# Four fused convolution layers on one Trainium2 core: other products placed elsewhere between an automaton's steps, and the parts of three pipelined layers in another order

## The chip, the cores and the metric

The kernel runs on one core of one Trainium2 chip. The metric is device time in microseconds (us) of one launch. TensorE is written PE, VectorE DVE, ScalarE ACT, GpSimd POOL and SyncE SP, as in the profile. SP and POOL issue the DMAs here. All matrix products are float32 with 512 columns unless said otherwise; the hardware runs such a product as two passes, and the profile counts passes.

## The reference

The input is 32 images of 8 channels and 256 by 256 pixels. Four layers follow one another, each as `x = x + layer(_gn(x))`, where `_gn` normalises over 4 groups of 2 channels.

```python
# layer 0: an automaton (a coupled map lattice), a small network, and a gate between them
grid = drive = x[:, :8]
for _ in range(15):
    mapped = 3.9 * grid * (1.0 - grid)
    local = conv3x3(mapped, K_local, groups=8)
    grid = 0.85 * (0.7 * mapped + 0.3 * local) + 0.15 * drive
cml = clip(grid, 0.0001, 0.9999)
nca = sigmoid(conv1x1(relu(conv3x3(x, Wp)), Wu))          # 8 -> 128 -> 8 channels
g = sigmoid(conv1x1(relu(conv3x3([x, cml, nca], Wg1)), Wg2))
out0 = g * cml + (1 - g) * nca
# layer 1: 3x3 convolution of values rounded to 127 steps; the scale needs the maximum over all images
# layer 2: 3x3 convolution with bias;  layer 3: 5x5 box filter per channel
```

Layer 1's scale is a maximum over the whole batch, so layer 0 has to be done for all images before layer 1 starts.

## The kernel before

**First part, layer 0.** One image after another goes through `lattice(b, ahead)`, which runs the automaton, and beside it a generator `gated()` makes everything else of layer 0 (the network and the gate) in small batches. The order of all instructions is written out by hand: inside `tc.manual_schedule()` every engine executes in the order in which the Python code emits.

The automaton keeps six of the eight channels on PE. A step handles them as three pairs (j = 0, 1, 2). For each pair PE multiplies the patch of each channel (`patch_sb` with `state`, L408, two products) and then the rim of each patch (`rings`, L410, two products that run side by side); DVE adds the drive in PSUM (L418); ACT squares the sum into the next `state` (L435). `spread(i)` then copies the rims of the patches into `rings` by twelve small DMAs on SP (L272): `spread(0)` after pair 1 for pairs 0 and 1, `spread(1)` after pair 2 for pair 2. The other two channels are computed on DVE with nine taps per step (L342), and two more SP DMAs, `edges()`, carry their border rows (`strip`). The pool `ps_c` has three PSUM buffers, and a step needs six tiles, so the second product of a pair waits until ACT has squared an earlier pair.

Before the first step of an image, DVE normalises it (L350), PE transposes it in 32 pieces (L366), ACT squares it into `state` (L387), SP spreads the rims, and ACT scales the drive (L392). After the last step PE transposes back (L450).

`lattice` is itself a generator. Each `yield` hands out an amount of PE time in us, and the driver spends it on `gated()`:

```python
                for k, gap in enumerate(lattice(b, ahead)):
                    ...
                    left += gap
                    while left > 0 and place[0] < place[1]:
                        left -= next(rest)
```

`place[0]` is the batch that `gated()` is in, `place[1]` the batch that it may not start. A batch is four products of `wp_sb` (L684, tile `ph`), four narrow ones of `wu_sb` (L661, tile `pn`), and every fourth batch a gate (L571 to L588, tiles `pg`, `pq`). ACT reads `ph` and writes `hh` (L689), `pq` and writes `gt` (L590). There are 32 batches for each image (`BATCHES`). The tiles `ph`, `pq` and the small `ps` share three PSUM buffers. The element-wise rest of a gate is put into `spare` and executed on DVE by `work(k)`; `errands` loads and normalises the next image ahead, one piece at each `next(ahead)`.

**Second part, layers 1 to 3.** A loop over `b` in `range(B + 3)` has layer 1 of image b, layer 2 of image b-1 and layer 3 of image b-3 in the same turn. First `layer3` runs in eight half groups, and after each of them come the `tasks` of that place: the steps of two statistics (`stats_parts`, L106 to L126), `quantize1` in four quarters (DVE and ACT), `normal2` (DVE, then two SP DMAs that fill `xb2`), `beside(..., qb, qh, 0)` (two SP DMAs that fill `qb`), and `by_group` (L136 to L140). Then `both()` alternates one block of `layer2` (L785, L789 with `xh`, `xb2`) and one of `layer1` (L785, L789 with `qh`, `qb`, in bfloat16). The last product of a `layer1` block reads `qb`.

Between the two parts the tiles of the second one are set to zero by six memsets on POOL (L779), and `top` (L155 to L167) finds the maximum. That stretch is outside `manual_schedule`, so the framework's scheduler interleaves it.

Of the kernel before, what the change touches and what calls it, by code (L numbers as in the profile page):

```python
# [22 lines left out]
HP, WP = H + 2, W + 2  # L23
# [27 lines left out]

SETS = ((0, 2), (2, 1))
RQ = 4
BLOCK = 12.6
STEPS = 15
R_, EPS_, BETA_ = 3.9, 0.3, 0.15

# [14 lines left out]
def kernel(  # L72
# [3 lines left out]
    nc = tc.nc  # L76
    B = x.shape[0]
# [54 lines left out]
    def by_group(psum, st):  # L132

        sel = small.tile([P, 4, 2], F32, name="sel")
        for j in range(2):
            nc.vector.tensor_scalar(sel[:, :, j], gsel_sb, st[:, j : j + 1], None, ALU.mult)  # L136
        ps = psum.tile([P, 512], F32, name="ps")
        nc.tensor.matmul(ps[:, 0:8], ones, sel.rearrange("p a b -> p (a b)"), start=True, stop=True)
        got = small.tile([P, 4, 2], F32, name="got")
        nc.vector.tensor_copy(got.rearrange("p a b -> p (a b)"), ps[:, 0:8])  # L140
        return got

    def beside(queue, t, src, q):

# [28 lines left out]
    with ExitStack() as es:  # L173
# [6 lines left out]
        psum = es.enter_context(tc.tile_pool(name="ps_a", bufs=3, space=PSUM))  # L180
# [151 lines left out]
        def lattice(b, ahead):  # L332
# [4 lines left out]
            st, st2 = sts[b % 2]  # L337
# [25 lines left out]
            for t4 in range(TX // 4):  # L363
                ps = psum.tile([P, 512], F32, name="ps")
                for j in range(4):
                    nc.tensor.transpose(  # L366
                        ps[:, bass.ts(j, P)], flat[:, bass.ts(4 * t4 + j, P)], eye_sb
                    )
                nc.scalar.copy(flat[:, bass.ts(t4, 512)], ps)
                if t4 == 4:  # L370
                    if b > 0:
                        store(b - 1)
                    place[1] = BATCHES * (b + 1) - (4 if b + 1 < B else 1)
                if t4 == 1:
                    nc.vector.tensor_scalar(
                        d2, d2, st2[:, 0:1], st2[:, 1:2], ALU.subtract, ALU.mult
                    )
                    nc.vector.scalar_tensor_tensor(own, d2, 1.0, d2, ALU.subtract, ALU.mult)
                    edges()
                if t4 > 1:  # L380
                    work(1)
                yield 1
            follow()
            dr = flat.rearrange("p (x c y) -> p c x y", x=TX, c=C)
            for i, cs in enumerate(((0, 3, 1, 4), (2, 5))):
                for c in cs:
                    nc.scalar.activation(inner(c), dr[:, c], AF.Square, bias=minus)  # L387
                spread(i)
                yield 1.5
            nc.scalar.mul(d2, d2, BETA_)  # L390
            for c in (0, 3, 1, 4, 2, 5):
                nc.scalar.activation(  # L392
                    dr[:, c], dr[:, c], AF.Identity, bias=lift[:, c : c + 1], scale=BETA_
                )
                yield 0.8
            yield 5.5


            taps_of = (((1, 0), (1, 1)), ((1, 2), (0, 0), (0, 1)), ((0, 2), (2, 0), (2, 1), (2, 2)))
            for step in range(STEPS):  # L400
                for j in range(PAIRS):
                    i = j // 2
                    mine = (j, PAIRS + j)
                    pss = []
                    for c in mine:
                        ps = ps_c.tile([P, 512], F32, name="psc")
                        pss.append(ps.rearrange("p (x y) -> p x y", y=TY))
                        nc.tensor.matmul(pss[-1], patch_sb[:, c, :], inner(c), start=True, stop=False)  # L408
                    for ps, base in zip(pss, (LOW, HIGH)):
                        nc.tensor.matmul(  # L410
                            ps, ring_sb[base : base + RING, j, :],
                            rings[i][base : base + RING, j - SETS[i][0], 0 : TX * SY].rearrange(
                                "p (x y) -> p x y", y=SY
                            )[:, :, 0:TY],
                            start=False, stop=True,
                        )
                    for c, ps in zip(mine, pss):
                        nc.vector.scalar_tensor_tensor(ps, ps, FLOOR, dr[:, c], ALU.max, ALU.add)  # L418
                    if step == STEPS - 1:
                        for c, ps in zip(mine, pss):  # L420
                            nc.vector.tensor_scalar(
                                dr[:, c], ps, 0.0001, 1.0 - 0.0001, ALU.max, ALU.min
                            )
                    for dy, dx in taps_of[j]:
                        tap(dy, dx)
                    end = j == PAIRS - 1
                    if end and step < STEPS - 1:
                        nc.vector.tensor_scalar(acc, acc, FLOOR, None, ALU.max)
                        nc.vector.scalar_tensor_tensor(own, acc, 1.0, acc, ALU.subtract, ALU.mult)
                    if end and step == STEPS - 1:  # L430
                        nc.vector.tensor_scalar(own, acc, 0.0001, 1.0 - 0.0001, ALU.max, ALU.min)
                    yield 0.8
                    if step < STEPS - 1:
                        for c, ps in zip(mine, pss):
                            nc.scalar.activation(inner(c), ps, AF.Square, bias=minus)  # L435
                        if j == SETS[i][0] + SETS[i][1] - 1:
                            spread(i)
                        if end:
                            edges()
                    if end:  # L440
                        work(4)
                    else:
                        next(ahead, None)
                    if j == 1:
                        follow()
                    yield BLOCK - 4.0 if end else 0.8
            for t4 in range(TX // 4):
                ps = psum.tile([P, 512], F32, name="ps")
                for j in range(4):
# [56 lines left out]
        place = [0, 0]  # L506
        BATCHES = 4 * NCH
# [231 lines left out]
    with ExitStack() as es:  # L739
        wt = es.enter_context(tc.tile_pool(name="wt1", bufs=1))  # L740
        two = es.enter_context(tc.tile_pool(name="two", bufs=2))
        psum = es.enter_context(tc.tile_pool(name="ps_b", bufs=3, space=PSUM))
# [32 lines left out]

        xr = wt.tile([P, 2, C, W + 4], F32, name="xr")
        xr2 = wt.tile([72, C, W + 4], F32, name="xr2")
        for t in (qh, qb, xh, xb2, xr, xr2):
            nc.gpsimd.memset(t, 0.0)  # L779

        def conv3(src, near, w, i):
            ps = ps_v.tile([P, 512], F32, name="psv")
# [36 lines left out]
        def normal2(x2, st):  # L819
            nc.vector.tensor_scalar(  # L820
                xh[:, :, 1 : 1 + W], x2.rearrange("p (k w) -> p k w", w=W),
                st[:, 0:1], st[:, 1:2], ALU.subtract, ALU.mult,
            )
            beside(nc.sync, xb2, xh, 0)
# [87 lines left out]
        def step(parts):  # L912
            return lambda: next(parts, None)
# [7 lines left out]
        with tc.manual_schedule():  # L921
            x1s[0] = load1(0)
            for b in range(B + 3):
                if b + 1 < B:
                    x1s[b + 1] = load1(b + 1)
                tasks = {i: [] for i in range(8)}
                if 2 <= b <= B + 1:
                    st3, parts3 = sums.pop(2)
                    for i in range(4):
                        tasks[i].append(step(parts3))  # L930

                    def groups():
                        gss[b - 2] = by_group(psum, st3)

                    tasks[5].append(groups)
                if 1 <= b <= B:
                    st, parts = sums.pop(1)
                    for i in range(4):
                        tasks[i].append(step(parts))
                    tasks[3].append(lambda: normal2(x2s[b - 1], st))  # L940
                if b < B:
                    for k in range(4):
                        tasks[k].append(lambda k=k: quantize1(b, x1s[b], k))
                    tasks[4].append(lambda: beside(nc.sync, qb, qh, 0))
                among(layer3(b - 3, ys.pop(b - 3)) if b >= 3 else iter(()), tasks)
                tasks = {}
                if 2 <= b <= B + 1:
                    for g in range(4):
                        tasks[g] = [lambda g=g: normal3(ys[b - 2], gss[b - 2], g)]
                    tasks[3].append(beside3)  # L950
                bns = [small.tile([P, NCH, 6], F32, name="bn") for _ in range(2)]
                if b < B:
                    x2s[b] = two.tile([P, NPX], F32, name="x2")
                ones_ = layer1(b, x1s[b], x2s[b], bns[0]) if b < B else iter(())

                def both():
                    for _ in layer2(b - 1, x2s[b - 1], bns[1]) if 1 <= b <= B else range(8):
                        next(ones_, None)
                        yield

                among(both(), tasks)
                if 1 <= b <= B:
                    sums[2] = begin(bns[1])
                    ys[b - 1] = load3(b - 1)
                if b < B:
                    sums[1] = begin(bns[0])
# [138 lines left out]
```

## Time and profile before

| | us |
|---|---|
| median of three runs (lowest, highest) | 16057.42 (16030.44, 16071.58) |
| the profiled execution | 16044.26 |
| its span, first to last instruction | 16042.5 |
| start of the normalisation (L350) of image 1, 11, 21, 31 | 402.5, 4527.0, 8666.8, 12808.0 |
| last gate products of the first part (L588) | 13318.95 |
| first product of the second part (L785) | 13351.71 |
| PE busy in 4000 to 8000 | 3784.99 |
| PE busy in 13300 to 13500 | 102.06 |
| PE busy in 13500 to 16042 | 2385.88 |

Starts of images in the middle lie about 414 us apart. A turn of the second part takes about 81 us. The span is 1.8 us shorter than the execution itself, so the two can be used for one another.

A line of groups in the profile reads: source line, engine, operation, output and inputs, shapes, count, busy time, mean ns, idle time before it and what ended it. A line of waits reads: who waited, for whom, us in total, how often, the longest. "PEclk" is the share of full clock speed that PE was granted.

### The profile page before, as it was taken

The page shows a single profiled execution, that of the slowest core. Times are in us where ns is not written, and L with a number is a line of the kernel's source. Part 1 is how long each engine was busy: PE and PEld are TensorE (multiplying, and loading weights), DVE is VectorE, ACT ScalarE, POOL GpSimd, SP SyncE. Part 2 cuts the span into 40 slices and gives each one's busy share as a digit, 9 for nine tenths or more (in the row PEclk, how much of TensorE's full clock was granted, in tenths as well). Part 3 has the DMA queues.
Part 4 walks back from the last instruction along what each step waited for, and adds up shares of the span by engine and source line. Part 5 has one row for each costly group of instructions (what it writes and reads, how often), then busy time and mean ns, then how long its engine had stood idle before and what let it go on. Part 6 is the DMA issues. An engine that isn't in the chain of part 4 may idle for free. (4 is left out here: it accounts for less than half of the span.)

```text
span 16042.5 us, 158554 instructions
## 1 busy us (share of the span) xinstructions
PE 15001.2 (94%) x42888; PEld 5437.6 (34%) x42888; DVE 11572.5 (72%) x14652; ACT 5754.6 (36%) x8864; POOL 5667.6 (35%) x9558
## 2 busy tenths in 40 slices
PE   7999999999999999999999999999999997999999
PEld 2333333333333333333333333333333333333333
DVE  7777777777777777777777777777777775555554
ACT  3444444444434444444434444444444431111110
POOL 3433333333433433334433333333333332111111
PEclk9999999999999999999999999999999998999999
DMA  5666666666666666666666666566656554555554
GB/s 128 149 148 148 148 146 144 146 147 147 149 146 145 150 144 148 147 147 150 146 144 145 143 146 148 141 149 145 146 145 145 142 143 106 119 117 119 120 118 106
DMA packets 1172088, 2248.19 MB, mean 140 GB/s; under 512 B 472477, under 2 KB 676373, under 8 KB 1164949
## 3 DMA queue, kind: packets, MB, share of 16 engines
q0 software_dynamic: 734208, 1628.10, 42.8%
q1 hardware_dynamic: 437012, 609.95, 15.8%
q8 instruction: 370, 6.06, 0.2%
q14 instruction: 498, 4.07, 0.1%
HBM read 1169.35 MB, written 539.02 MB: 106 GB/s over the span
## 5 line engine op out<-in xcount | busy, mean ns | idle before, releaser
L342 DVE SCALAR_TENSOR_TENSOR acc<-strip,taps_sb,acc 128x1024 f32<-128x1024 f32 x3840 | 4925.9, 1283 | 485.2 <-DMA strip<-strip 387.4
L540 POOL DMA_DIRECT2D im<-xn_d x6144 | 3483.8, 573 | 4640.2 <-PE ph L684 3775.8
L684 PE MATMUL ph<-im,wp_sb 72*128 72x512 f32 x8192 | 4269.2, 635 | 269.3 <-ACT hh L689 126.5
L689 ACT ACTIVATE hh<-ph,bp_sb 128x512 f32<-128x512 f32 x4096 | 2758.0, 688 | 3778.2 <-PE ph L684 3726.1
L418 DVE SCALAR_TENSOR_TENSOR psc<-psc,flat 128x512 f32<-128x512 f32 x2880 | 1871.5, 693 | 2524.4 <-PE psc L410 2517.8
L408 PE MATMUL psc<-state,patch_sb 128*128 128x512 f32 x5760 | 2931.1, 623 | 163.0 <-ACT state L435 157.6
L435 ACT ACTIVATE state<-psc,minus 128x512 f32<-128x512 f32 x2688 | 1723.7, 689 | 3137.9 <-DVE psc L418 2756.2
L684 PEld LDWEIGHTS ph<-im,wp_sb 72*128 72x128 f32 x8192 | 1439.8, 195 | 2677.8 <-issue 1971.7
L410 PE MATMUL psc<-rings,ring_sb 56*128 56x512 f32 x5760 | 1805.7, 650 | 230.9 <-DMA rings<-state 212.6
L408 PEld LDWEIGHTS psc<-state,patch_sb 128*128 128x128 f32 x5760 | 1041.7, 194 | 1904.1 <-issue 1249.6
L871 PE MATMUL psv<-xr,w_sb 128*128 128x512 f32 x2560 | 1163.0, 600 | 1.3 <-DVE xr L852 1.3
L661 PE MATMUL pn<-hh,wu_sb 128*32 128x512 f32 x8192 | 1138.1, 624 | 0.0
L836 POOL DMA_DIRECT2D x_d<-x x512 | 324.9, 650 | 1944.5 <-DVE x L830 1703.1
L410 PEld LDWEIGHTS psc<-rings,ring_sb 56*128 56x128 f32 x5760 | 485.4, 187 | 1436.0 <-issue 1037.1
L571 PE MATMUL pg<-cq,wg_sb 128*128 128x512 f32 x1536 | 772.8, 642 | 0.0
L785 PE MATMUL psv<-xh,w_sb 128*128 128x512 f32 x1536 | 750.1, 627 | 9.6 <-issue 9.6
L571 PE MATMUL pg<-xq,wg_sb 128*128 128x512 f32 x1536 | 741.7, 620 | 0.0
L814 ACT ACTIVATE x<-psv,b_sb,sc 128x512 f32<-128x512 f32 x256 | 199.0, 777 | 1461.6 <-PE psv L789 1440.9
L562 POOL DMA_DIRECT2D xc<-xr_d x256 | 145.7, 569 | 1554.5 <-DVE ext L603 673.2
L871 PEld LDWEIGHTS psv<-xr,w_sb 128*128 128x128 f32 x2560 | 466.1, 189 | 610.9 <-issue 606.0
L342 DVE SCALAR_TENSOR_TENSOR acc<-strip,taps_sb,d 128x1024 f32<-128x1024 f32 x480 | 612.4, 1276 | 0.0
L891 DVE TENSOR_TENSOR y<-psv,y 128x512 f32<-128x512 f32 x256 | 177.1, 692 | 591.8 <-PE psv L871 591.8
(165 smaller groups left out, 12207.9 us busy)
## 6 DMA issues: line engine op xcount, KB each, us to landing
im<-xn_d POOLq DMA_DIRECT2D x6144, 96.6 KB, 4.4
rings<-state SPq DMA_DIRECT2D x1920, 70.1 KB
strip<-strip SPq DMA_DIRECT2D x960, 126.0 KB
rings<-state SPq DMA_DIRECT2D x1920, 35.1 KB
xn_d<-xb POOLq DMA_DIRECT2D x128, 516.0 KB, 11.3
nh_d<-nh POOLq DMA_DIRECT2D x256, 258.0 KB, 5.4
nr_d<-xb POOLq DMA_DIRECT2D x128, 516.0 KB, 7.0
xq<-nr_d POOLq DMA_DIRECT2D x128, 516.0 KB, 5.7
```

The costliest lines, as they stand in the source:

```text
L342: nc.vector.scalar_tensor_tensor(acc, strip[:, dy : dy + RQ, dx : dx + W], taps_sb[:, 3 * dy + dx : 3 * dy + dx + 1], d2 if dy == 1 and dx ...
L408: nc.tensor.matmul(pss[-1], patch_sb[:, c, :], inner(c), start=True, stop=False)
L410: nc.tensor.matmul(ps, ring_sb[base : base + RING, j, :], rings[i][base : base + RING, j - SETS[i][0], 0 : TX * SY].rearrange("p (x y) -> ...
L418: nc.vector.scalar_tensor_tensor(ps, ps, FLOOR, dr[:, c], ALU.max, ALU.add)
L435: nc.scalar.activation(inner(c), ps, AF.Square, bias=minus)
L540: nc.gpsimd.dma_start(im[24 * dy : 24 * dy + 24, k, 0:run], window(xn_d[b % 3], at, [[HP * WP, C], [1, 3], [1, run]]),)
L571: nc.tensor.matmul(o, wg1_sb[:, s, dx, :], src[:, :, dx : dx + W], start=s == dx == 0, stop=False,)
L661: nc.tensor.matmul(pn[32 * q : 32 * q + 32, :], wu_sb[:, i, :], hh, start=i == 0, stop=i == 3,)
L684: nc.tensor.matmul(ph.rearrange("p (k w) -> p k w", w=W), wp_sb, im[:, :, j * WP : j * WP + W], start=True, stop=True,)
L689: nc.scalar.activation(hh, ph, AF.Relu, bias=bp_sb)
L785: nc.tensor.matmul(o, w[:, dx, :], src[:, 2 * i : 2 * i + 2, dx : dx + W], start=dx == 0, stop=False,)
L871: nc.tensor.matmul(pss[k].rearrange("p (c w) -> p c w", w=W), w3_sb[:, dx, :], xr[:, k, mine, dx : dx + W], start=dx == 0, stop=stop,)
```

## The change

1. `BLOCK` goes from 12.6 to 12.2: the PE time handed out in a step. After pairs 0 and 1, 1.6 is handed out in place of 0.8; after pair 2, what is left of the block, 6.6 in place of 8.6.
2. Ahead of the first step, 11 is handed out in place of 5.5.
3. `gated()` has to stop two batches earlier at the end of an image (6 in place of 4 before the end), and may use these batches from the start of the next image on. For image 0 it may start only after the squares, no longer amid the transposes.
4. The six whole memsets on POOL become one on POOL (`xr2`), two whole ones on DVE (`qb`, `xb2`), and small ones on DVE for the borders of `qh`, `xh` and `xr`.
5. `by_group` becomes a generator with a pause between its DVE and its PE part.
6. In a turn of the second part the statistics of layer 1 come first and in three places in place of four, `normal2` comes one place earlier, the quarters of `quantize1` and the DMAs of `qb` get other places, the statistics of layer 2 come one place later each, and the PE part of `by_group` has two more half groups ahead of it.
7. `layer1` starts two blocks after `layer2`, and its last two blocks follow at the end.

```diff
-BLOCK = 12.6
+BLOCK = 12.2
 def by_group(psum, st):
         for j in range(2):
             nc.vector.tensor_scalar(sel[:, :, j], gsel_sb, st[:, j : j + 1], None, ALU.mult)
+        yield None
         ps = psum.tile([P, 512], F32, name="ps")
...
-        return got
+        yield got
 def lattice(b, ahead):
                 if t4 == 4:
                     if b > 0:
                         store(b - 1)
-                    place[1] = BATCHES * (b + 1) - (4 if b + 1 < B else 1)
+                        place[1] = BATCHES * (b + 1) - (6 if b + 1 < B else 1)
...
                 spread(i)
                 yield 1.5
+            if b == 0:
+                place[1] = BATCHES - 6
             nc.scalar.mul(d2, d2, BETA_)
...
-            yield 5.5
+            yield 11
...
-                    yield BLOCK - 4.0 if end else 0.8
+                    yield BLOCK - 5.6 if end else 1.6
 second part:
-        for t in (qh, qb, xh, xb2, xr, xr2):
-            nc.gpsimd.memset(t, 0.0)
+        for t in (qh, xh):
+            for w in (0, WP - 1):
+                nc.vector.memset(t[:, :, w : w + 1], 0.0)
+        for t in (qb, xb2):
+            nc.vector.memset(t, 0.0)
+        for k in range(2):
+            for w in (0, W + 2):
+                nc.vector.memset(xr[:, k, :, w : w + 2], 0.0)
+        nc.gpsimd.memset(xr2, 0.0)
...
+                if 1 <= b <= B:
+                    st, parts = sums.pop(1)
+                    for i in (0, 1, 1, 2):
+                        tasks[i].append(step(parts))
+                    tasks[2].append(lambda: normal2(x2s[b - 1], st))
                 if 2 <= b <= B + 1:
                     st3, parts3 = sums.pop(2)
                     for i in range(4):
-                        tasks[i].append(step(parts3))
+                        tasks[i + 1].append(step(parts3))
+                    parts4 = by_group(psum, st3)
+                    tasks[4].append(step(parts4))
 
                     def groups():
-                        gss[b - 2] = by_group(psum, st3)
-
-                    tasks[5].append(groups)
-                if 1 <= b <= B:
-                    st, parts = sums.pop(1)
-                    for i in range(4):
-                        tasks[i].append(step(parts))
-                    tasks[3].append(lambda: normal2(x2s[b - 1], st))
+                        gss[b - 2] = next(parts4)
+
+                    tasks[6].append(groups)
                 if b < B:
                     for k in range(4):
-                        tasks[k].append(lambda k=k: quantize1(b, x1s[b], k))
-                    tasks[4].append(lambda: beside(nc.sync, qb, qh, 0))
+                        tasks[(0, 2, 2, 3)[k]].append(lambda k=k: quantize1(b, x1s[b], k))
+                    tasks[3].append(lambda: beside(nc.sync, qb, qh, 0))
...
                 def both():
-                    for _ in layer2(b - 1, x2s[b - 1], bns[1]) if 1 <= b <= B else range(8):
-                        next(ones_, None)
+                    twos = layer2(b - 1, x2s[b - 1], bns[1]) if 1 <= b <= B else iter(range(8))
+                    for i, _ in enumerate(twos):
+                        if i > 1:
+                            next(ones_, None)
                         yield
+                    for _ in ones_:
+                        pass
```

## The prediction

> **What bounds the kernel now.** I read the page first, for the engine that is full:
>
> ```profile
> PE 15001.2 (94%) x42888; PEld 5437.6 (34%) x42888; DVE 11572.5 (72%) x14652; ACT 5754.6 (36%) x8864; POOL 5667.6 (35%) x9558
> PEclk9999999999999999999999999999999998999999
> ```
>
> PE is busy 94% of the span. The program's products are the same before and after, so time can only come from PE's idle 1041 us and from its clock: the view of the cores gives a mean granted clock of 0.960, so 4% of 16042.5, 642 us, went to half speed. Who PE waits for is in the view of waits for PE (waiter, releaser, us in total, times, longest):
>
> ```profile
> PE psc L410 <- DMA rings<-state: 212.6, 78, 6.3
> PE psc L408 <- ACT state L435: 157.6, 289, 2.9
> PE ph L684 <- ACT hh L689: 126.5, 88, 5.6
> PE psv L789 <- DMA qb<-qh: 123.1, 31, 13.5
> PE ph L684 <- ACT gt L590: 103.2, 24, 7.6
> PE ps L116 <- DVE t L113: 49.6, 62, 1.0
> PE ps L138 <- DVE sel L136: 45.5, 32, 12.9
> ```
>
> Then the timeline of PE at the first step of image 10, and the windows (length, PE busy, ..., clock, DMA share, GB/s) over it:
>
> ```profile
> 4145.44 1.88 PE L408 MATMUL psc<-state,patch_sb 128*128 128x512 f32 x4
> 4147.25 1.12 PE L410 MATMUL psc<-rings,ring_sb 56*128 56x512 f32 x2
> 4154.69 2.04 PE L410 MATMUL psc<-rings,ring_sb 56*128 56x512 f32 x2 [6.32 <-DMA rings<-state]
> 4156.66 3.78 PE L684 MATMUL ph<-im,wp_sb 72*128 72x512 f32 x4
> ```
>
> ```profile
> 4145.40:4154.70 9.30, 2.98 (x8) 0.90 (x6) 0.70 (x1) 0.69 (x1) 4.65 (x9) 0.91 0.84 166
> 4154.70:4165.70 11.00, 11.00 (x22) 3.04 (x22) 3.17 (x3) 3.11 (x5) 5.75 (x11) 0.61 0.87 232
> ```
>
> PE waits 6.3 us for the rims, and then pays again: four passes take 3.78 us, where 1.9 is usual. I cut the trace of images 3 to 29 at the first L408 of each step. An image takes 414.0 us, with 22.7 idle and 16.2 lost to the clock, so 375 would be PE's floor. Step 0 holds 5.2 of the idle (26 of the 27 images wait for rims) and 5.4 of the clock loss. Step 1 holds 2.1 and 3.2, step 4 (`gt`) 3.4 and 2.7, step 13 (`hh`) 2.9 and 1.6. In the second part, one turn:
>
> ```profile
> 14533.40 1.02 PE L789 MATMUL psv<-xb,w_sb 72*128 72x512 f32 x2
> 14534.26 0.81 PE L785 MATMUL psv<-qh,w_bf 128*128 128x512 bf16 x3
> 14540.20 0.61 PE L789 MATMUL psv<-qb,w_bf 72*128 72x512 bf16 x1 [5.13 <-DMA qb<-qh]
> 14540.61 4.04 PE L785 MATMUL psv<-xh,w_sb 128*128 128x512 f32 x6
> ```
>
> The same six passes take 2.74 us two blocks later: a slow spell again.
>
> **The Trainium skill.** "TensorE: Matmul & The Clock Gate", Part 1, says that the array falls to half clock after an idle activity window of about 3.4 us and returns after a busy one. The trace agrees on the window (all half-speed spells are multiples of 3.41 us) but needs less idleness: of 107 such windows with PE busy under half, 106 were followed by half speed; busy 0.6 to 0.7, 26%; over 0.75, none. About 1.3 us of idle in a window is enough, so a wait costs itself plus 1.7 us or more. "VectorE: DVE Perf Modes", on zero memsets, gives a memset one cycle per element; at the 0.96 GHz of its Specifications I estimate 4.3 us for 4128 elements (the 128-element memset at L93 took 0.165 us here). "GPSIMD Engine Reference", 1. Specifications, says that POOL shares its SBUF interfaces with VectorE; during POOL's memsets this trace has
>
> ```profile
> 13328.79 11.95 DVE L629 TENSOR_SCALAR ext<-ext,stat 128x2 f32<-128x2 f32 x1
> ```
>
> where the same operation elsewhere takes 0.29 us.
>
> **The change part by part.** Products are counted in the built program's order on PE, before against after, at 0.857 us each (two passes of 0.4285), narrow ones at 0.26.
>
> *Ahead of step 0.* Between the last transposes and the first L408 stand 13.8 us of other products before, 17.7 to 21.1 (mean about 19.2) after. The rims' chain (squares, twelve SP issues, landing) is emitted ahead of this filler and doesn't move; at 40.7 us after the image's start the rims are there in either version. So 5.4 us of filler stands where 4.6 us of waiting for rims stood. Idle falls by 4.7, and with it nearly all of the clock loss, 5.0: **-9.7 us an image**. Its `im` loads come earlier on POOL, by one batch; POOL is busy a third of the time.
>
> *Between the pairs.* The mean filler after pairs 0 and 1 goes from 1.8 and 1.1 to 2.3 and 2.4, after pair 2 from 9.4 to 7.1. The L408 waits (0.3 to 0.8 us in nine steps, 4.6 an image) stand where no filler follows the pair before; those places nearly vanish: **-4.0**. L116 (1.6 an image) waits for four short DVE operations behind taps; 0.8 more filler: **-1.2**. The `hh` and `gt` waits in steps 3, 4 and 13 (6.4 idle, 5.9 clock) come from DVE being late for pair 2, so that ACT stands at L435 with `hh` and `gt` queued behind it; pair 2 now comes later relative to pair 1. I take half: **-6.3**.
>
> *What is late next.* From pair 1's last product to the next step's rim products PE had 16.1 us of work, now 15.1 (mean of the order). In it must fit DVE 2.0, ACT 0.7, twelve SP issues of 8.1 (up to 11.9 when DMA is crowded) and the landing. PE came 6.0 us (median of calm steps) after the last issue, now 5.0. Each SP issue waits for the DMA eight earlier, and in calm steps runs unhindered at 0.68, so landing takes under 5.4 us there. In the crowded steps 1, 3, 5, 9 and 14 the margin is gone: idle +3.5, clock +2.0: **+5.5**. Bounds: 0 to +20. `edges()` stand behind both spreads on SP and keep their distance (a whole step, 0.4 shorter).
>
> Sum: -15.7, I take -15 for each of images 2 to 31: **-450**.
>
> *First images, end of the part.* The two batches more that are held back change little at the image's border: 6.2 us of filler stand among the first transposes before, 6 to 8 after, and a gate's loads of `cq` get two batches more after their store. Images 0 and 1 hold 8.9 and 6.0 us less filler. After image 31, 18.3 us more remain, which nothing hides. In image 0 the transposes no longer stand behind a `ph` that waits 16.4 us for `im`; most of that wait only moves: I take -4 (0 to -12). Together **0**, -10 to +10.
>
> *Between the parts.* The 11.95 us of L629 go. On DVE 4.3 (`xb2`) and 2.1 (`qb`) come into the same chain, and the load of `x1`, issued on POOL behind the memsets before, is no longer waited for (2.3 us). With `normal2` earlier in turns 1 and 2, some 3 and 5 us: **-15**, 0 to -30.
>
> *The turns.* In 28 full turns PE waited 109.2 us for `qb` (3.9 each) and 29.4 for `sel` (1.05), and lost about 1.85 to the clock. After, `xb2`'s DMA is issued about 9 us earlier, `qb`'s 2.5 us earlier behind it on SP's queue, and its first reader comes two layer-2 blocks, 6.9 us, later: 9.4 us more against 5.1 at most. `sel` gets 9.8 us between its parts. New: three layer-1 blocks end the turn in 2.6 us of PE, while DVE needs 1.4 for each, so the statistics at L109 come about 0.9 late, under what trips the clock. Sum -5.9 a turn, times 29: **-171** (-110 to -200). `normal2` and the quarters only change places on DVE, which is busy 56%. On SP the order stays `xb2`, `qb`, output; on POOL the sixteen stores of layer 2 leave 1.7 us earlier, ahead of the last layer-1 blocks, and nobody waits for them in the turn.
>
> Total: -450 - 0 - 15 - 171 = -636, on 16044 (0.1% under the median of runs): 15,408, **about 15,410 us**.
>
> **Rivals.** *B, the map's waits move.* Step 0 is filled, but SP's chain takes back the rest, step 1 above all: -5 an image, 15,710. For it: DMA share 0.87 to 0.89 around steps 0 and 1. *C, more than half goes.* Image 1, whose batches fall otherwise, ran steps 0 to 13 in 23.1 us each against 24.8 later; with that the image gains 23: 15,170. For it: the order now drifts against the steps, so no stall recurs in every image. *D, slower.* Rims late in every step: if landing takes 7 us after the last issue, each of 14 steps waits 2.0 and loses 1.0 to the clock, 42 an image, less the 21.2 gained elsewhere, on 30 images, less 186: about 16,480. It decides from 27.4 us an image, 2.0 a step, a landing of some 6.3 us. Calm steps speak against it; in step 1 the landing did take a median 6.2. *E, no change*: the order on PE shows the products moved, so only a balance of B and D gives it.
>
> **How the numbers follow.** A 0.50, B 0.22, C 0.18, D 0.07, E 0.03. A alone spans 15,270 to 15,560: a quarter more or less of the image's 15 (4 us, 120 over 30 images), and 20 to 30 for the turns. The range leaves out D, E and the ends of B and C: 15,230 to 15,770. Within 0.3% (48 us) a measurement can't tell it from no change: faster 0.90, same 0.03, slower 0.07.
>
> **What would show it.** Right: images 399 us apart; rims' waits in step 0 under 1 us, half-speed spells there gone, mean clock near 0.98; waits of L408 for L435 under 40 us in all; turns of 75.5 us without a wait for `qb` or `sel`, about 25 us at L109 in all; the multiplication of `ext` under 1 us. Wrong: rims waited for in most steps, images at 409 or more, or turns over 78 us.

## The result, and the profile after

The changed kernel takes 15,827.36 us (median of four runs, 15,772.5 to 15,863.16) against 16,047.08 for the kernel before in the same comparison: a ratio of 0.9867, 95% interval 0.9849 to 0.9886. The forecast was 15,410, with 15,230 to 15,770 as its range. The sign was right; the gain was about 220 us where 636 were expected. The profiled execution took 15,801.65 us with a span of 15,799.9.

Two lines of the page after, PE's busy time and its granted clock:

```profile
PE 14977.6 (95%) x42888; PEld 5479.2 (35%) x42888; DVE 11527.8 (73%) x14662; ACT 5680.6 (36%) x8838; POOL 5669.9 (36%) x9553
PEclk8999999999999999999999999999999998999999
```

PE's idle time fell from 1041 to 822 us, nearly all of the 243 us by which the span is shorter. The mean clock stayed at 0.960, where 0.98 was forecast. The view of waits for PE (waiter, releaser, us in total, times, longest; code lines have moved by three in most places, so L413 was L410, L411 was L408, L438 was L435, L687 was L684) tells which idle time went:

```profile
PE psc L413 <- DMA rings<-state: 237.2, 133, 4.5
PE psc L411 <- ACT state L438: 96.1, 93, 3.2
PE ph L687 <- ACT gt L593: 62.7, 38, 6.1
PE ph L687 <- DMA im<-xn_d: 61.6, 22, 16.9
PE ps L109 <- DVE mv L106: 53.1, 35, 27.5
...
PE ph L687 <- ACT hh L692: 38.1, 34, 6.0
...
PE psv L796 <- ACT x L825: 26.1, 30, 0.9
...
PE ps L116 <- DVE t L113: 13.2, 10, 5.0
...
PE psv L800 <- DMA qb<-qh: 11.7, 1, 11.7
PE ps L139 <- DVE sel L136: 11.4, 1, 11.4
```

`hh`, `gt`, L116 and the waits for the squared state fell by 88, 41, 36 and 62 us, and `qb` and `sel` by 111 and 34. The rims did not follow: 212.6 us in 78 waits became 237.2 in 133. Of the 212.6, 118 were in step 0, where no image has any now; elsewhere 94 us became 237.

The timeline of PE in image 10 after, with a step whose rims come late, and the windows over it (length, PE busy, ..., clock, DMA share, GB/s):

```profile
4153.49 1.12 PE L413 MATMUL psc<-rings,ring_sb 56*128 56x512 f32 x2
4158.92 2.07 PE L413 MATMUL psc<-rings,ring_sb 56*128 56x512 f32 x2 [4.31 <-DMA rings<-state]
4160.92 2.07 PE L687 MATMUL ph<-im,wp_sb 72*128 72x512 f32 x2
4162.93 1.94 PE L664 MATMUL pn<-hh,wu_sb 128*32 128x512 f32 x8
4164.79 3.23 PE L411 MATMUL psc<-state,patch_sb 128*128 128x512 f32 x4
```

```profile
4151.60:4160.90 9.30, 4.99 (x9) 1.36 (x7) 2.18 (x3) 1.38 (x2) 2.28 (x5) 0.80 0.83 183
4160.90:4168.00 7.10, 7.10 (x17) 1.92 (x16) 3.17 (x3) 1.38 (x2) 4.55 (x8) 0.55 0.86 220
```

It is the picture that step 0 showed before (a wait of 6.3 us, then 11 us at clock 0.61), now in step 2: 4.3 us of waiting, then 7.1 us at clock 0.55, in which two passes of L687 take 2.07 us, and four of L411 take 3.23 where 1.9 is usual.

Cut at the first product of each step, images 3 to 29 show per image (us; "clock loss" is half of the time at half speed; here and below "rims" are PE's waits for DMA `rings`):

| | before | after |
|---|---|---|
| whole image | 413.97 | 409.72 |
| idle, clock loss | 22.7, 16.2 | 19.0, 16.6 |
| start to end of step 0: idle, clock loss | 6.05, 5.37 | 2.68, 1.45 |
| steps 1 to 14: idle, clock loss | 15.6, 10.0 | 14.0, 13.5 |
| idle of step 1, of step 2 alone | 2.10, 0.77 | 2.14, 2.13 |
| transposes back: idle, clock loss | 1.13, 0.82 | 2.31, 1.64 |

What was saved ahead of step 0 was partly given back in steps 1 to 14 and at the transposes back, mostly in the clock.

The second part did what was forecast: from the end of the last gate product to the end it takes 2558.3 us, 2722.4 before. A turn is 76.3 us (81.5 before, 75.5 forecast), and its first layer-1 products no longer wait for `qb`. In the middle turns two waits are left, in this timeline of PE (one turn; only the lines with a wait are shown):

```profile
14321.90 2.84 PE L796 MATMUL psv<-xh,w_sb 128*128 128x512 f32 x6 [0.87 <-ACT x L825]
14340.55 0.38 PE L109 MATMUL ps<-mv,gavr_sb 128*128 128x1 f32 x2 [0.29 <-DVE mv L106]
```

The multiplication of `ext`, 11.95 us beside POOL's memsets before, takes 0.29 in all of its 32 places (group: busy us, mean ns, idle before):

```profile
L632 DVE TENSOR_SCALAR ext<-ext,stat 128x2 f32<-128x2 f32 x32 | 9.3, 289 | 1.1
```

### The profile page after: what moved, and what is told of

Same layout as the page of the kernel before. It is cut to its first block, busy times and chain, and to the rows that moved or that the text cites. A ratio compares the mean times of both kernels' runs of the same rounds, so it can differ in the third digit from the quotient of the medians.

```text
span 15799.9 us, 158467 instructions
## 1 busy us (share of the span) xinstructions
PE 14977.6 (95%) x42888; PEld 5479.2 (35%) x42888; DVE 11527.8 (73%) x14662; ACT 5680.6 (36%) x8838; POOL 5669.9 (36%) x9553
## 3 DMA queue, kind: packets, MB, share of 16 engines
q1 hardware_dynamic: 437012, 609.95, 16.6%
## 5 line engine op out<-in xcount | busy, mean ns | idle before, releaser
L687 PE MATMUL ph<-im,wp_sb 72*128 72x512 f32 x8192 | 4303.8, 638 | 210.1 <-ACT gt L593 62.7
L411 PE MATMUL psc<-state,patch_sb 128*128 128x512 f32 x5760 | 2898.2, 623 | 103.5 <-ACT state L438 96.1
L438 ACT ACTIVATE state<-psc,minus 128x512 f32<-128x512 f32 x2688 | 1717.8, 687 | 2908.6 <-DVE psc L421 2495.4
L687 PEld LDWEIGHTS ph<-im,wp_sb 72*128 72x128 f32 x8192 | 1434.0, 195 | 2601.6 <-issue 2102.2
L413 PE MATMUL psc<-rings,ring_sb 56*128 56x512 f32 x5760 | 1861.7, 652 | 257.6 <-DMA rings<-state 237.2
L411 PEld LDWEIGHTS psc<-state,patch_sb 128*128 128x128 f32 x5760 | 1087.3, 197 | 1787.2 <-issue 1328.5
L413 PEld LDWEIGHTS psc<-rings,ring_sb 56*128 56x128 f32 x5760 | 499.6, 188 | 1511.2 <-issue 1049.6
L847 POOL DMA_DIRECT2D x_d<-x x512 | 374.4, 747 | 1400.9 <-DVE x L841 1176.2
L796 PE MATMUL psv<-xh,w_sb 128*128 128x512 f32 x1536 | 711.6, 599 | 32.4 <-ACT x L825 26.1
L432 DVE SCALAR_TENSOR_TENSOR strip<-acc 128x1024 f32<-128x1024 f32 x448 | 549.8, 1227 | 15.3
```

The lines of the kernel that those rows point to most:

```text
L413: nc.tensor.matmul(ps, ring_sb[base : base + RING, j, :], rings[i][base : base + RING, j - SETS[i][0], 0 : TX * SY].rearrange("p (x y) -> ...
L687: nc.tensor.matmul(ph.rearrange("p (k w) -> p k w", w=W), wp_sb, im[:, :, j * WP : j * WP + W], start=True, stop=True,)
L796: nc.tensor.matmul(o, w[:, dx, :], src[:, 2 * i : 2 * i + 2, dx : dx + W], start=dx == 0, stop=False,)
```

## The experiments

All ratios are to the kernel before, measured beside it on the same chip; brackets hold the 95% interval. "Images apart" is the mean from image 2 to image 31. The first four take the change apart.

**The second part alone** (items 4 to 7 of the change on the kernel before).

```diff
-BLOCK = 12.2
+BLOCK = 12.6
-            yield 11
+            yield 5.5
-                    yield BLOCK - 5.6 if end else 1.6
+                    yield BLOCK - 4.0 if end else 0.8
 and the two lines with BATCHES - 6 as before
```

> The second part of the change alone (memsets, the parts of layers 1 to 3), the automaton as before. Theory 1 (the two halves of the change add up; from the last gate product to the end the trace fell from 2713.8 to 2549.7 us): 164 us less than before, about 15,883, turns of 76.3 us. Theory 2 (the second part profits from the first, by batches left for its start): clearly less than 130 us.

Measured: 15,875.05 us, 0.9892 (0.9877 to 0.9907). The second part took 2557.8 us, as in the whole change. So about 173 us of the gain are its own, and only some 40 to 55 are the first part's, where the forecast had 450. One more thing is to be read here: this kernel's first part is that of the kernel before, and its image 2 started at 824.0 us, as in the changed kernel (826.2), where the profile of before had 802.6. Two executions of the same first part thus differ by nearly as much as the 24 us that the first two images seemed to lose, and nothing is built on it.

**The first part alone** (items 1 to 3).

> The automaton's part of the change alone (block of 12.2, 1.6 after pairs 0 and 1, 11 ahead of the first step, two batches more held back, image 0 starting later), layers 1 to 3 as before. Theory 1: the rest of the gain, 56 to 80 us less than before, about 15,980; images in the middle 409.7 us apart against 414. Theory 2 (this part gains nothing for certain): within 0.3% of before.

Measured: 16,003.43 us, 0.9966 (0.9957 to 0.9976); images 411.1 us apart where 409.7 was expected; the interval leaves both theories open. The two halves add within their intervals: 0.34% and 1.08% against 1.33%.

**Only the filler ahead of step 0.**

```diff
-BLOCK = 12.6
+BLOCK = 12.2
-            yield 5.5
+            yield 11
```

> Only the block of 12.2, handed out as 0.8, 0.8 and the rest, with 11 ahead of the first step; the spacing of pairs and the batches held back as before. Theory 1 (the filler ahead of step 0 pays, the spacing of the pairs takes it back through the rims): images gain at step 0 some 7 us (idle and clock together) and lose little elsewhere, 407 us apart or less, 150 to 250 us less than before. Theory 2 (what is filled at step 0 comes back in step 1 whatever the spacing): 409 to 413 us apart, under 120 us less.

Measured: 15,880.05 us, 0.9892 (0.9877 to 0.9906); images 406.7 us apart. Up to the end of step 0 an image saves 4.0 us of idle and 3.8 of clock loss, 7.8 where 9.7 was forecast; steps 1 and 2 take back 1.2. This one edit brings more than the whole first part of the change.

**Only the spacing of the pairs.**

```diff
-                    yield BLOCK - 4.0 if end else 0.8
+                    yield BLOCK - 5.6 if end else 1.6
```

> Only the spacing of the pairs: 1.6 after pairs 0 and 1 and 7.0 after pair 2, in a block of 12.6; 5.5 ahead of the first step and the batches held back as before. Theory 1 (short waits of L408 that do not trip the clock are traded for waits for rims that do): idle of steps 1 to 14 about the same, clock loss higher, the images 414 us apart or more, time from 0 to 120 us more than before. Theory 2 (the spacing helps, the loss is elsewhere): 60 us or more less than before.

Measured: 16,169.63 us, 1.0077 (1.0063 to 1.0090), slower; images 417.3 apart, clock 0.947. Its waits for PE:

```profile
PE psc L410 <- DMA rings<-state: 294.8, 119, 7.2
PE ph L684 <- DVE st L330: 137.5, 29, 4.7
...
PE psc L408 <- ACT state L435: 61.9, 48, 2.6
```

The forecast's short waits of L408 did go, from 157.6 us in 289 places to 61.9 in 48. In their place the rims' waits grew by 82 us, and a wait of `ph` for the next image's statistics (L330; their `ps` shares its buffers with `ph`) came to 137.5 us, 4.7 in step 11 of each image. That step alone went from 22.8 to 29.5 us, more than the 3.3 by which the image grew: in this kernel the later rims are only a part of the cost. An image's clock loss rose from 16.2 to 22.3 us, 3.8 of it in step 11. Steps 2 and 7 to 11, which held little but short waits before, lost no clock then; the steps with the long waits do.

**The change without the spacing and the longer hold** (the second part, and the filler ahead).

```diff
-                        place[1] = BATCHES * (b + 1) - (6 if b + 1 < B else 1)
+                    place[1] = BATCHES * (b + 1) - (4 if b + 1 < B else 1)
-            if b == 0:
-                place[1] = BATCHES - 6
-                    yield BLOCK - 5.6 if end else 1.6
+                    yield BLOCK - 4.0 if end else 0.8
```

> The whole change without its wider spacing between the pairs and without the two batches more held back. Theory 1 (gains add: the filler ahead of step 0 is worth about 181 us, the second part about 186, and the spacing gives about 109 back): 15,700 us (15,660 to 15,740), images 406.7 apart, second part 2550. Rival (the spacing costs only when it stands alone with the old block, and in the whole change costs nothing; then this kernel is as the changed one): 15,800 to 15,850.

Measured: 15,715.35 us, 0.9797 (0.9782 to 0.9811); images 406.3 apart. It is faster than the changed kernel by 112 us, with nothing but edits of the change left out. The additive theory holds. The edit takes out the spacing and the longer hold together; the next kernel parts them.

**The change with four batches held back instead of six.**

```diff
-                        place[1] = BATCHES * (b + 1) - (6 if b + 1 < B else 1)
+                    place[1] = BATCHES * (b + 1) - (4 if b + 1 < B else 1)
-            if b == 0:
-                place[1] = BATCHES - 6
```

> The changed kernel with four batches held back as before, in place of six, and free to use them amid image 0's transposes. Theory 1 (the spacing costs the 112 us between the changed kernel and the one without spacing and hold): within 25 us of the changed kernel, 15,800 to 15,850. Rival (holding back costs it, by waits at the image's border): 15,700 to 15,740.

Measured: 15,914.57 us, 0.9911 (0.9895 to 0.9928); images 414.2 apart. Neither theory has it. Against the kernel without spacing and hold, the spacing costs 199 us by the medians (183 by the ratios), more than was thought; and holding back two batches more, which the forecast put at nothing, brings 87 (70) of them back. With the spacing the rims' waits rise from 134.3 to 255.9 us; PE's idle time rises by only 1.6 us an image, but the clock loss by 8.3 (12.3 to 20.6).

**The rims' chain, shortened.** The next kernels ask whether twelve issues on SP, one after another, are what PE meets. The view of the tile `rings` on SP in the trace after (count: duration in ns, lowest, median, highest):

```profile
L273 SPq DMA_DIRECT2D rings<-state x11520: 542/654/3328, 45.2 to 13069.8; - x199
```

Twelve of these take about 8 us. The first kernel leaves out the corner rims (the two DMAs of each side that carry four rows each), so eight issues remain.

```diff
-                for q, n, p, step, far, m, by in RINGS:
+                for q, n, p, step, far, m, by in RINGS[:4]:
```

> The changed kernel without the two DMAs of each side that bring the corner rims (eight SP issues in place of twelve for each spread; the corners stay zero, so that part of the map is left out). Theory 1 (the rims' chain on SP is what the spacing runs into): the chain is some 2.7 us shorter, waits for rims fall from 237 us to under 70, the half speed behind them goes too, images 401 to 405 apart, 15,550 to 15,680 us. Rival 1 (PE only comes sooner to the next late thing, hh, gt or the states): rims' waits fall but others rise as much, images 408 to 410, 15,780 to 15,830. Rival 2 (rims are late because the DMA engines are crowded, not because of the issues): rims' waits stay over 150 us, 15,750 or more.

Measured: 14,930.42 us, 0.9305 (0.9291 to 0.9318), 897 us under the changed kernel and far under every expectation; images 381.2 apart, clock 0.984. Its waits for PE:

```profile
PE psc L411 <- ACT state L438: 118.7, 102, 4.2
...
PE ph L687 <- ACT gt L593: 13.1, 27, 1.2
...
PE psc L413 <- DMA rings<-state: 6.1, 11, 1.5
```

The rims are hardly waited for any more, and idle and clock loss of an image fall from 19.0 and 16.6 to 7.0 and 3.6. That is 25 of the 28 us by which it is shorter; in the other 3 PE's products take less time, clock loss apart, and why is open. The waits for `gt` went with the rims' (62.7 to 13.1 us).

Are the corner DMAs slow themselves, with four rows each? The semaphore updates in the trace after tell when each of SP's DMAs landed:

| rows of the DMA (pairs 0 and 1) | count | issue to landing, us: median | 90% under |
|---|---|---|---|
| 16 | 1920 | 4.51 | 7.95 |
| 8 | 1920 | 4.20 | 7.72 |
| corners, 4 | 1920 | 4.16 | 7.61 |

They land as fast as the others. In 470 of the 480 spreads of pairs 0 and 1 the DMA that was issued last landed last; from the first issue to the last landing it took a median of 12.2 us, and 9.2 without the corners. The row of issues itself fell from 8.5 to 5.3 us, while the landing after the last issue stayed (3.3 and 3.6). So what shortens the chain is the number of issues in the row, and not that there are fewer bytes in flight; the next two kernels move the same bytes and gain as well.

**The same DMAs, the corners issued by POOL.**

```diff
-                    nc.sync.dma_start(
+                    (nc.sync if m == 1 else nc.gpsimd).dma_start(
```

> The changed kernel with the corner rims issued by POOL in place of SP: the same DMAs, eight of twelve on SP. Theory 1 (SP's issues set the landing, and POOL is free most of the time): most of what leaving them out brings, 15,580 to 15,720 us, waits for rims under 100 us. Rival (the corners stand behind loads and stores on POOL's queue that wait for something): rims later than before, waits over 300 us, 15,900 or more.

Measured: 15,354.66 us, 0.9571 (0.9557 to 0.9585), better than expected. The rims' waits are still 175.8 us, but in other places: 4.0 us an image in step 2 and 0.9 in step 0, and next to none in steps 7 to 14. That loads ahead of them on POOL's queue are the reason is not shown.

**The corners by POOL, except where POOL is busy.**

```diff
-        def spread(i):
+        def spread(i, other):
...
-                    nc.sync.dma_start(
+                    (nc.sync if m == 1 else other).dma_start(
...
-                spread(i)
+                spread(i, nc.sync)
...
-                            spread(i)
+                            spread(i, nc.sync if step == 1 else nc.gpsimd)
```

> The changed kernel with the corner rims issued by POOL, but by SP ahead of step 0 and in step 1, where POOL's queue stood behind its loads (in the run before this, step 2 waited 4.0 us for them and step 0 0.9). Theory 1: step 2 falls to the changed kernel's own 2.1 of idle and 2.3 of clock loss, step 0 to 0.6 and 0.6, so 6 to 9 us an image less: 15,080 to 15,200. Rival (POOL's queue is late elsewhere then, or SP's later issues are): 15,330 or more.

Measured: 15,254.33 us, 0.9502 (0.9485 to 0.9518); images 392.0 apart, rims' waits 108.6 us in 48 places. It leaves nothing out, and beats the kernel before by 792 us and the changed one by 573; it is the best of the complete kernels here. It falls short of its expectation by 54 us at least: step 2 still waits 2.2 us an image, and step 6 0.8.

**The corners by ACT.**

```diff
-                    nc.sync.dma_start(
+                    (nc.sync if m == 1 else nc.scalar).dma_start(
```

> The changed kernel with the corner rims issued by ACT in place of SP, whose queue has no loads in it. Theory 1: the chain on SP is 2.7 us shorter in every step, waits for rims under 60 us, 15,000 to 15,200 us. Rival (eight issues a step of about 0.7 us stand ahead of hh, gt and the next squares on ACT): hh, gt and state waits over 300 us together, 15,400 or more.

Measured: 16,440.30 us, 1.0247 (1.0229 to 1.0265). The rival is right. In the view of the tile `rings` on ACT, who waited for these issues:

```profile
L273 ACTq DMA_DIRECT2D rings<-state x3840: 624/626/2567, 45.1 to 13698.3; - x192
...
  ACT hh L692: 1823.6, 629
```

Eight issues of 0.63 us a step stand ahead of `hh` on ACT. The rims' waits halve, to 112.6 us, but PE's waits for `hh` and `gt` go from 101 to 806. An engine that is busy 36% of the time is not free for issues when other engines wait on its order.

**Does the clock follow the waits?** The changed kernel with the two state products of pair 0 made twice in steps 1 and 2.

```diff
-                        nc.tensor.matmul(pss[-1], patch_sb[:, c, :], inner(c), start=True, stop=False)
+                        for last in (False, True) if j == 0 and step in (1, 2) else (True,):
+                            nc.tensor.matmul(pss[-1], patch_sb[:, c, :], inner(c), start=True, stop=not last)
```

> The changed kernel with the two state products of pair 0 made twice in steps 1 and 2 of the map, with the same result: 3.4 us more PE work in each image, placed ahead of the rim products that wait there. Theory 1 (a wait for rims of 1.7 us costs itself and then a half-speed spell): the work takes the place of the waits in steps 1 and 2 (3.3 us) and of most of the clock loss there (5.2), so -2 to -5 us an image, 15,680 to 15,770 us, although PE does more. Rival 1 (the chain of rims sets the step, the clock does not matter): within 20 us of the changed kernel. Rival 2 (PE sets the step, and all later work shifts): +3.4 on 32 images, about 15,930.

Measured: 15,795.01 us, 0.9852 (0.9836 to 0.9868). The intervals of this and of the changed kernel overlap, so the time alone decides only against rival 2: 110 us more of products did not make it slower. The traces say more. Steps 1 and 2 together lose 2.0 us of idle and 2.1 of clock loss an image, and gain 3.4 of work, -0.9 in sum (the two steps fall from 54.3 to 53.4 us). Each microsecond of waiting that was filled took one of half-speed loss with it. That the clock loss goes with the wait is theory 1's, at about half the size. But the two steps keep nearly their length, as rival 1 has it (the chain sets the step), and this run doesn't decide between the two.

**The first part with the short chain.** Three more kernels leave out the corner rims, to see what the edits are worth where the chain doesn't bind: the kernel before, the kernel without spacing and hold, and the one with the spacing but without the hold. Each has the edit of `RINGS[:4]` shown above.

> The kernel before without the corner rims (that part of the map is left out). Theory 1 (the forecast's gains ahead of step 0 and between the pairs were right, about 20 us an image, and only the chain took them back): images 396 to 402 apart against 381.2, 15,560 to 15,720 us. Rival (much of the forecast gain was itself the chain's, in step 0 above all, and goes with it): the filler ahead is then worth some 4 us an image and the spacing 4, images 387 to 391 apart, 15,300 to 15,440 us.

> The second part and the filler ahead of step 0, with the old spacing and four batches held back, and without the corner rims (that part of the map is left out), to stand beside the changed kernel without corner rims (14,930). Theory 1 (the wider spacing does what the forecast said of hh, gt and the state waits, and costs only through the rims' chain): without the chain the old spacing is the slower one, 15,000 to 15,130 us, images 384 to 387 apart, hh, gt and state waits over 250 us together (147 in the other). Rival (the spacing brings nothing even then): 14,900 to 14,950.

> The changed kernel with four batches held back, without the corner rims. Theory 1 (the hold only moves the batches against the steps, and so decides in which steps the rims are late): with the short chain it makes no difference, 14,900 to 14,960 us. Rival (it saves work or waits at the image's border): some 90 us slower, 15,000 to 15,040.

| edits in place | all rims: us, ratio | images apart | no corners: us, ratio | images apart |
|---|---|---|---|---|
| none (before) | 16,047, 1 | 414.0 | 15,142.68, 0.9438 (0.9425 to 0.9451) | 383.3 |
| second part, filler ahead | 15,715.35, 0.9797 | 406.3 | 15,064.31, 0.9387 (0.9372 to 0.9402) | 385.1 |
| and spacing | 15,914.57, 0.9911 | 414.2 | 15,037.71, 0.9367 (0.9353 to 0.9382) | 385.4 |
| and hold (the whole change) | 15,827.36, 0.9867 | 409.6 | 14,930.42, 0.9305 (0.9291 to 0.9318) | 381.2 |

The kernel before gains 903 us from the shorter chain alone, below both of its expectations. Its waits for PE then read:

```profile
PE psc L408 <- ACT state L435: 160.7, 292, 4.2
...
PE ph L684 <- ACT hh L689: 25.5, 33, 0.9
...
PE psc L410 <- DMA rings<-state: 6.9, 4, 2.5
PE ph L684 <- ACT gt L590: 1.9, 1, 1.9
```

Three things follow from the table. First, with a short chain the second part still brings 173 us (2733.0 to 2559.9 in the traces), which leaves about 40 of the 212 us for the first part's three edits: they had little to gain but what the chain had caused. Second, the filler ahead of step 0 (with its smaller block) then costs rather than gains: 78 us less in all where the second part alone brings 173, and 385.1 against 383.3 an image. Third, the spacing, which costs 199 us with twelve issues, makes 27 us less with eight, within the overlap of the intervals: its price on top of the other edits is the chain's. The expectation of `ahead_no_corners` is met by its number, but not by its reason, since `no_hold_no_corners` puts most of the 134 us down to the hold. That edit brings 107 us there and 87 with all rims, so it doesn't work by where the rims are late. In the short-chain kernels most of its 4.2 us an image lie among the transposes back (15.3 to 12.3 us from the first to the last), where PE's waits for DVE's copy (`xb`, at the `ph` products) fall from 38.6 to 11.8 us in all; with all rims that stretch changes little (15.3 to 14.7), and the gain lies in other steps. How the hold works there stays open.

## Why the prediction was wrong

**What bounds the kernel: half right.** PE's idle time and clock were the right place to look, and a wait followed by half speed the right unit. But for `hh` (126.5 us) and `gt` (103.2) the reading stopped at DVE being late for pair 2. Why DVE was late, and what else held ACT, stands in the waits of the kernel before:

```profile
DVE acc L342 <- DMA strip<-strip: 387.4, 140, 7.7
ACT state L435 <- DMA rings<-state: 369.0, 143, 8.7
```

DVE's taps wait for `strip`, whose two DMAs (`edges()`) are issued by SP behind both spreads, and ACT may not overwrite `state` before the spreads have read it. Followed back wait by wait through the trace, 103 us of the `gt` waits and 60 of the `hh` waits end at `strip`, and 48 more of `hh` at ACT's wait for `rings`. With four issues fewer in a spread, and DVE's work unchanged, the two lines above become 12.1 us in 11 waits and 73.3 in 45, and `hh` and `gt` 25.5 and 1.9. So the row of SP issues was behind them as well as behind the rims. The releaser that a view of waits names is the last link; what made that link late was not followed back. (Half of 6.4 and 5.9 is also 6.15, not the 6.3 of the forecast, which changes nothing.)

**Ahead of step 0, forecast -9.7: nearly right.** Alone it gives -7.8 up to the end of step 0, and -7.3 on the image. In the whole change -7.3 are left up to the end of step 0 (3.4 of idle, 3.9 of clock).

**Between the pairs, -11.5, and what is late next, +5.5: the steps that failed.** Their sum of -6.0 an image came out as +3.3 alone, and +7.9 on top of the other edits. Alone, part of that is the wait in step 11 that the forecast did not have; on top of the other edits that wait is nearly gone (9.4 us in all), and the rims and the clock behind them make the difference. The direction of each wait was right: the short waits for L408 went as forecast (157.6 to 96.1 us in the whole change, though under 40 was hoped for), L116 as well, and `hh` and `gt` together fell by half, as taken (229.7 to 113.5 us with the spacing alone). The price of the rims was not. The prediction took PE's lead over the last issue (from its end to the rim products) as 6.0 us, 5.0 after, and let the landing exceed it in five named steps only. Measured in the traces, the lead in the steps without a wait was a median of 6.0 before and fell to 4.3 or 4.4. After its last issue the chain landed within a median 3.2 us in both kernels, but 90% only within 7.2 before and 6.7 after. Landing later than the lead of 6.0 happened in 15% of the steps before; later than 4.4, in 25% of the steps after. Nor do the crowded steps stay where they were: before, the landing was slowest in steps 1 and 14 (medians 8.3 and 7.5 us), after in step 2 (7.8). The five steps named in the forecast have 1.9 us of rims' waits an image after; steps 2, 4, 6, 10 and 11, which were not named, have 4.9. A change of block and spacing drifts the loads against the steps, so a list of steps read from the trace before cannot be kept.

**The clock, the largest single miss.** Of the forecast 15 us an image, about 6 were clock: 5.0 in step 0, 2.9 with `hh` and `gt`, less 2.0. Measured is +0.4. It was gained in step 0 (3.9) and lost again in steps 1 to 14 (3.5) and at the transposes back (0.8). Of the 289 state waits before (157.6 us, at most 2.9 long and mostly half a microsecond), 2 had a half-speed spell begin during them or within 2 us after; of the 133 rims' waits after, 83 had, together 191 us, with 580 us at half speed, so 290 us were lost on top. The idle window of about 3.4 us that the Trainium skill names, page "TensorE: Matmul & The Clock Gate", Part 1, need not be idle throughout: 47 of the 50 rims' waits over 2 us were followed by half speed, and 13 of the 43 under 1 us. The forecast's "about 1.3 us is enough" is too firm beside its own 26%: at that length it is a chance, near certain only when half the window is idle (106 of 107). The forecast knew of the rule, and still priced waits by their length when it traded one kind for the other.

**First images and end of the part, 0: wrong in one part.** Holding back two batches more was put at nothing; it is worth 70 to 87 us, and how is open. After image 31 about 25 us more remain, 18.3 forecast.

**Between the parts, -15, and the turns, -171: right.** -164 in the trace: 5.1 us in each of 29 turns, 149, and 15 elsewhere, 11.4 of it between the parts, where the first layer-2 product comes 61.1 us after the last gate product, 72.5 before. The memset of 4128 elements, estimated at 4.3 us, took 3.50. What made L629 slow before is only in part shown: it ended with the last of POOL's memsets (13340.7), but other DVE operations beside the first of them kept their time (L610 at 13322.3: 0.69 us). The turn misses its forecast by 0.8 us. The wait that was foreseen at the end of the turn came at the next layer-2 product (0.87 us for `x`) rather than at L109, where 0.29 is left in most turns.

**The rivals.** B, "the map's waits move", named this mechanism and 15,710; it was the nearest. D named the landing, with a bound that held: not every step is late. C's hope, that the image could fall by 23 us and more, was right for the kernel and wrong for the edit: it falls by 31 when the chain is shortened by leaving the corners out.

## What to carry to other kernels

Before pricing a gap that is filled or widened, follow each frequent wait back to the start of its chain, and compare the whole distribution of that chain's time, its slow tenth above all, with the slack that the edit leaves; a median in calm stretches says nothing about who trips. A row of small DMA issues on one queue is a serial stage like any other: count issues times duration, and try to take some out of the row, or give them to a queue with nothing urgent in it, before moving work around it. And trade waits by what they do to the clock, not by their length.

## What was not expected of the hardware

- The number of issues counted, not the bytes: four fewer of twelve (0.65 us each on SP) make the chain 3.0 us shorter, and the image 28 to 31 us. A page of the Trainium skill, "Perfetto Trace Analysis", section "DMA Instruction — HWDGE (DVE, Sync)", says that the duration shown for such a DMA is not its data movement; the trace agrees: 0.65 us of issue, and medians of 4.2 to 4.5 from issue to landing (pairs 0 and 1).
- The same issue takes 0.63 us on ACT, where it blocks ACT's other work, and 0.54 on POOL (median).
- Two executions of the same first part had image 2 start 21 us apart (802.6 and 824.0).
